# Reciprocals swapped between halves of the partitions, one row tile normalised before the last division, and own rows of the output projection interleaved

## The chip, the cores and the metric

The kernel runs on one core of a Trainium2 chip. The metric is the device time of one execution in microseconds. Five engines work beside each other: TensorE (PE, with its weight loads shown as PEld), VectorE (DVE), ScalarE (ACT), GpSimd (POOL) and SyncE (SP), which here only issues DMAs.

## The reference

x has 64 graphs of 256 nodes with 512 features; adj is one 256x256 graph for all of them. Two layers follow each other, each with a residual and a layer norm over the features:

```python
# layer 0
mi = einsum('bkd,od->bko', x, Wi);  mj = einsum('bkd,od->bko', x, Wj)
deg = adj.sum(axis=1)
x = layernorm(x + deg[None, :, None] * (mi + b) + einsum('ij,bjo->bio', adj, mj))
# layer 1: 8 heads of 64
q, k, v = split_heads(x @ Wq.T + bq), split_heads(x @ Wk.T + bk), split_heads(x @ Wv.T + bv)
scores = where(adj == 0, -inf, q @ k^T / 8)
attn = softmax(scores, axis=-1)
x = layernorm(x + concat_heads(attn @ v) @ Wo.T + bo)
```

## The kernel before, in words

**Tiles.** The 64 graphs are worked on in 32 groups g of two graphs. A graph has two row tiles of 128 nodes (t = 0, 1) and four chunks of 128 features (c = 0 to 3). The residual stream of a graph is xh[b], 128 partitions x 2 x 512.

**Main loop.** It has 31 trips. Trip g does the attention of group g and, between its steps, layer 0 of the two graphs of the next group (b1 and b2). Then come the output projection of group g and the values, queries and keys of group g+1. The order of instructions on each engine is the order in which the program calls the steps: `in_order` pins it. Every engine works through its own list, and semaphores hold it where it needs another engine's result. Pools of buffers add waits: a tile that takes a buffer waits for the last reader of the tile before.

**Three-part products.** A large product (values, queries, keys, output) is made from three fp32r products. Its left operand is split into a head (ACT, `split_head`, L665), a difference (DVE, `split_diff`, L668) and a low part (POOL or DVE, `split_low`, L671); the weights have been split in the same way into `factor` tiles, 768 KB each, which ACT's queue streams from DRAM through a ring of 6 (`bring`, L442). Heads and lows add up in one PSUM bank X, differences in another, Y (`rows_of_product`). ACT and DVE, or DVE alone, join the two: for the output projection, `add_x` (L811) and `add_y` (L815) add X and Y to xh. All matmuls have the line of a helper, L290, so one tells them apart by their tiles.

**Banks.** Pairs X, Y come from three places: "S" takes a score pair (pool of 2 pairs, tile pxy), "M" takes two of the 3 banks of the mm pool (px, py), and "A" takes one mm bank and the one value bank (py). The mm pool also serves layer 0 (po) and the denominators (den); the value bank also serves attention's output (pav).

**Parts of the attention output.** aoT holds the output of the group before the projection: four chunks, columns of graph 0 (own rows, n = 0, 1 by row tile) and of graph 1 (other rows, n = 2, 3). Its head lies in tile qT, its difference in kT, its low part in v, since those buffers are free then. Upper means chunks 0 and 1, lower chunks 2 and 3. Lower of graph 1 comes out of the last division of the trip.

**Division.** Softmax isn't normalised before the product with the values. `values` fills pav for two chunks; `divide_two` copies pav to aoT (ACT, L931) and calls `divide`. That sums each denominator over the keys on TensorE (den, 128 rows in groups of 32), takes the reciprocal on DVE (rden, L974), and spreads it with four DMAs of 64x256 from SBUF to SBUF (L979), so that each row of both chunks has its own reciprocal. SP issues the four, but in the last division of a trip ACT issues two of them. `multiply` then multiplies aoT by spread on POOL (L925). `total` sums rden on ACT for a check at the end.

**Normalisation and transposition of h.** `stat` takes the mean and variance of a row tile on DVE (L474 to L480) and the root on POOL (rstd, L482), and `give` scales the row tile on ACT (shift L487, xh L488). `send_h` stores the row tile to DRAM in column blocks (L687), `fetch_h` loads it back (hB, L692), and `turn_h` transposes it in blocks on DVE (hF, L506); SP issues both DMAs. h10 and h11 are row tiles 0 and 1 of b1. The row tiles of b2 are turned inside the output projection.

**The steps around the change**, in the order of the program: values 6 and 7 of the trip; low part of graph 0; statistics of row tile 1 of b2; last division; statistics of row tile 0; low part of graph 1, upper; scaling of both row tiles; store and fetch of both; then the output projection, with row 0, row 1 and the other rows as three steps, and the values product of the next group.

Of the kernel before, what the change touches and what calls it, by code (L numbers as in the profile page):

```python
# [16 lines left out]
P = 128  # L17
# [207 lines left out]
def unshifted_path(ctx, tc, flag, x, adj, wiT, wjT, b0, wqT, bq, wkT, bk, wvT, bv, woT, bo, out):  # L225
# [149 lines left out]
    def channels(q):  # L375

        half, j = divmod(q, 2)
        return slice(j * DH + half * R, j * DH + (half + 1) * R)

    def load_wo(t, c0):  # L380
        w = woT.rearrange("(c p) o -> p c o", p=P)
        for q in range(P // R):
            in_order(nc.sync.dma_start(out=t[q * R:(q + 1) * R], in_=w[channels(q), c0:c0 + t.shape[1], :]))

    def small_loads():
        with nc.allow_non_contiguous_dma(reason="512 numbers, once"):
            for q in range(P // R):
                in_order(nc.sync.dma_start(out=bv_t[q * R:(q + 1) * R],
                                           in_=bv.rearrange("r (c p) -> p (r c)", p=P)[channels(q)]))
        in_order(nc.sync.dma_start(out=bo_bc, in_=bo.to_broadcast([P, D])))  # L390
        return load_bias(bq, "bq"), load_bias(bk, "bk")

# [410 lines left out]
                    v_evict(g, i, t, banks[t])  # L803
        return run

    def o_steps(g, kinds, turn):
        parts = aoP[g]

        def add_x(i, t, banks):
            r = xh[NB * g + i][:, t, :]  # L810
            in_order(nc.vector.scalar_tensor_tensor(r, banks[0], UP, r, ALU.mult, ALU.add))  # L811

        def add_y(i, t, banks):
            r = xh[NB * g + i][:, t, :]
            in_order(nc.vector.tensor_add(r, banks[1], r))  # L815

        def one(t):
            def run():
                banks = pair(kinds[t])
                for which in ((0, 1), (2,)):  # L820
                    for c in range(NC):
                        rows_of_product(banks, parts, t, coming[c], c, which)
                add_x(0, t, banks)
                add_y(0, t, banks)
            return run

        def two():
            banks = [pair(kinds[NT + t]) for t in range(NT)]
            for c in range(NC):
                for which in ((0, 1), (2,)):  # L830
                    for t in range(NT):
                        rows_of_product(banks[t], parts, NT + t, coming[0], c, which)
# [8 lines left out]
            add_x(1, 0, banks[0])  # L841
            split_diff(*h1)
            add_y(1, 0, banks[0])
            add_x(1, 1, banks[1])
            add_y(1, 1, banks[1])
            split_three(*turn(0), nc.gpsimd)

        return [one(0), one(1), two]

    def finish_steps(g):  # L850

# [56 lines left out]
    def values(g, w):  # L908
        i, pr = divmod(w, NC)
        if w == 0:  # L910
            aoT[g] = p1.tile([P, NC, NB * N], F32, tag="aoT", name="aoT")
        pp = w % 2
        if pp == 0:
            pavs[g] = value_bank("pav").rearrange("p (r q) -> p r q", r=2)
        pe, _ = made[g, w]
        for kc in range(NT):
            for q in range(P // R):
                d0 = 2 * pr * DH + channels(q).start
                matmul(pavs[g][q * R:(q + 1) * R, pp, :], vv[g][:, i, kc, d0:d0 + R], pe[:, q % 2, kc, :],
                       start=(kc == 0), stop=(kc == NT - 1), tile_position=(0, q * R))  # L920

    def multiply():
# [4 lines left out]
    def divide_two(g, w):  # L927

        dst = target(g, w)
        last = w == NB * NC - 1 and g < NG - 1  # L930
        in_order(nc.scalar.copy(dst, pavs[g]))  # L931
        i, pr = divmod(w, NC)
        return divide(dst, [made.pop((g, w - 1))[1], made.pop((g, w))[1]],
                      rtot[:, NB * g + i, pr // 2:pr // 2 + 1], last)

    def total(rden, total_out):
        unused = p1.tile([P, N], F32, tag="unused", name="unused")
# [2 lines left out]
    def divide_at_once(g, w):  # L940


        den = score_bank("den").rearrange("p (r q) -> p r q", r=2)
        for pp in range(2):
            _, pk = made.pop((g, w - 1 + pp))
            for q in range(P // R):
                matmul(den[q * R:(q + 1) * R, pp, :], ones[:, :R], pk[:, q % 2, :], start=True, stop=True,
                       tile_position=(0, q * R))
# [12 lines left out]
        cols = slice(i * N, (i + 1) * N)  # L961
        return cut_parts(aoP[g], cs, cols), aoT[g][:, cs, cols]

    def divide(dst, pks, total_out, last):


        den = bank("den")[:, :N]
        for pp in range(2):
            for j in range(2):
                q = 2 * pp + j  # L970
                matmul(den[q * R:(q + 1) * R, :], ones[:, :R], pks[pp][:, j, :], start=True, stop=True,
                       tile_position=(0, q * R))
        rden = p1.tile([P, N], F32, tag="rden", name="rden")
        in_order(nc.vector.reciprocal(rden, den))  # L974
        spread = p1.tile([P, 2, N], F32, tag="spread", name="spread")
        for half in range(2):
            for pp in range(2):
# [131 lines left out]
    for g in range(NG - 1):  # L1109
# [214 lines left out]
```

## Time and profile before

| what | before |
|---|---|
| median of 3 runs | 2985.07 us (2984.91 to 2987.25) |
| the profiled execution | 2979.46 us, of which the span of the program's instructions is 2977.2 us |
| TensorE busy | 2934.5 us, 15694 matmuls, granted clock 0.998 |
| VectorE busy | 2310.1 us |
| GpSimd busy | 1273.0 us |
| ScalarE busy | 1194.6 us |
| DMA | 609.48 MB, 205 GB/s on average |

Busy times are sums over the whole span. Matmuls overlap each other in the records, so a busy TensorE is read by the distance from one start to the next, not by the length of a row. In a list of waits, each line names the engine and tile that waited, what ended the wait, the total in us, how often, and the longest. In a timeline, each row has its start in us, its length, the engine, the line, the operation with its tiles, and in brackets the idle time of the engine before it and who ended it.

### The profile page before, as it was taken

The numbers are of one execution on the slowest core, as the hardware profiler recorded it, in microseconds if no ns is written. First come the engines' busy times: TensorE is split into PE (matmuls) and PEld (weight loads), VectorE is DVE, ScalarE is ACT, GpSimd is POOL, SyncE is SP. The second block draws the span as 40 slices with busy tenths as digits, with TensorE's granted clock in tenths as the row PEclk, the third lists the DMA queues.
The fourth block names the chain that finished last, engine by engine and source line by source line (L and its number), as shares of the span: only waits on it lengthen the run. The fifth ranks groups of instructions, "written<-read, shape, count | busy, mean of one in ns | idle before, by whom it ended". The sixth has DMA issues, their size and how long they took to land. (4 is left out here: it accounts for less than half of the span.)

```text
span 2977.2 us, 42690 instructions
## 1 busy us (share of the span) xinstructions
PE 2934.5 (99%) x15694; PEld 1917.7 (64%) x15694; DVE 2310.1 (78%) x3497; ACT 1194.6 (40%) x2243; POOL 1273.0 (43%) x950
## 2 busy tenths in 40 slices
PE   9999999999999999999999999999999999999998
PEld 5566666666666666666666666666666666666655
DVE  5977787777887778877778777788777787777875
ACT  3433434434434334343343343443433434334333
POOL 3534444344444344443444444444434444344443
PEclk9999999999999999999999999999999999999999
DMA  6566655667555665556665566755566555666553
GB/s 230 172 231 237 217 162 185 222 234 240 178 179 197 235 239 202 167 188 229 236 237 164 177 211 231 245 184 170 197 237 238 201 160 191 232 237 236 166 167 125
DMA packets 305604, 609.48 MB, mean 205 GB/s; under 512 B 27632, under 2 KB 189424, under 8 KB 305136
## 3 DMA queue, kind: packets, MB, share of 16 engines
q10 hardware_dynamic: 75808, 391.02, 34.5%
q1 hardware_dynamic: 229584, 215.69, 25.1%
q8 instruction: 126, 2.06, 0.3%
q14 instruction: 86, 0.70, 0.1%
HBM read 494.67 MB, written 78.64 MB: 193 GB/s over the span
## 5 line engine op out<-in xcount | busy, mean ns | idle before, releaser
L897 POOL TENSOR_TENSOR pk<-pe 128x512 f32<-128x512 f32 x256 | 330.7, 1303 | 534.6 <-ACT pe L887 534.6
L290 PE MATMUL po<-w,xS 128*128 128x512 f32 x992 | 466.1, 602 | 1.5 <-DVE mj L570 1.5
L290 PE MATMUL po<-w,xT 128*128 128x512 f32 x808 | 387.4, 604 | 0.8 <-ACT u L549 0.8
L482 POOL TENSOR_TENSOR rstd<-ve,mhalf 128x1 f32<-128x1 f32 x256 | 155.3, 607 | 493.1 <-DVE below L480 491.9
L887 ACT ACTIVATE pe<-pe 128x1024 f32<-128x1024 f32 x256 | 270.6, 1057 | 148.2 <-DVE pe L883 148.2
L671 POOL TENSOR_TENSOR hL<-hF,hA 128x512 fp32r<-128x512 f32 x93 | 151.2, 1626 | 387.5 <-ACT hA L665 387.5
L290 PEld LDWEIGHTS po<-w,xS 128*128 128x128 f32 x992 | 177.8, 189 | 214.6 <-issue 162.2
L883 DVE TENSOR_TENSOR pe<-ps,maskT 128x1024 f32<-128x1024 f32 x256 | 300.9, 1196 | 3.6 <-PE ps L290 3.6
L759 DVE TENSOR_TENSOR kT<-py,kT 128x512 f32<-128x512 f32 x128 | 88.5, 691 | 259.7 <-ACT kT L758 259.7
L290 PEld LDWEIGHTS po<-w,xT 128*128 128x128 f32 x808 | 145.6, 189 | 180.5 <-issue 179.0
L367 POOL TENSOR_TENSOR xh<-xh,degb 128x1024 f32<-128x1024 f32 x64 | 152.4, 2382 | 254.9 <-DMA xh<-in_x_dram 134.8
L290 PE MATMUL ps<-qT,kT 64*128 64x256 f32 x2048 | 256.5, 389 | 0.0
L290 PE MATMUL pav<-pe,v_sb 128*32 128x256 f32 x4096 | 248.7, 382 | 3.5 <-DVE kT L759 1.5
L290 PEld LDWEIGHTS ps<-qT,kT 64*128 64x128 f32 x2048 | 187.0, 186 | 69.0 <-PE pav L290 38.7
L487 ACT ACTIVATE shift<-below,rstd 128x1 f32<-128x1 f32 x256 | 74.5, 291 | 386.3 <-POOL rstd L482 231.2
L974 DVE RECIPROCAL rden<-den 128x256 f32<-128x256 f32 x127 | 221.9, 1747 | 6.3 <-PE den L290 3.8
L290 PEld LDWEIGHTS pav<-pe,v_sb 128*32 128x32 f32 x4096 | 118.3, 109 | 155.4 <-issue 49.2
L488 ACT ACTIVATE xh<-xh,shift,rstd 128x512 f32<-128x512 f32 x256 | 208.9, 816 | 8.5
L925 POOL TENSOR_TENSOR aoT<-aoT,spread 128x512 f32<-128x512 f32 x127 | 205.7, 1620 | 6.9 <-DMA spread<-rden 5.9
L665 ACT ACTIVATE hA<-hF 128x512 fp32r<-128x512 f32 x124 | 77.8, 628 | 287.1 <-DVE hF L506 231.5
L290 PE MATMUL px<-hA,factor 128*128 128x512 f32 x640 | 184.3, 410 | 0.0
L290 PE MATMUL py<-hD,factor 128*128 128x512 f32 x640 | 176.3, 397 | 2.2 <-ACT kT L758 2.2
(142 smaller groups left out, 6060.1 us busy)
## 6 DMA issues: line engine op xcount, KB each, us to landing
factor<-wv ACTq DMA_DIRECT2D x124, 768.0 KB, 6.3
factor<-wq ACTq DMA_DIRECT2D x124, 768.0 KB, 6.6
factor<-wk ACTq DMA_DIRECT2D x124, 768.0 KB, 6.4
factor<-wo ACTq DMA_DIRECT2D x120, 768.0 KB, 7.2
xB<-in_x_dram SPq DMA_DIRECT2D x256, 128.0 KB, 3.7
xh<-in_x_dram SPq DMA_DIRECT2D x64, 512.0 KB, 8.9
h_cols<-xh SPq DMA_DIRECT2D x124, 256.0 KB, 2.3
hB<-h_cols SPq DMA_DIRECT2D x124, 256.0 KB, 3.1
```

Of the source, the lines that this page charges most:

```text
L290: in_order(nc.tensor.matmul(*args, **kw))
L367: in_order(nc.gpsimd.tensor_tensor(xh[b], xh[b], degb, ALU.add))
L482: order(nc.gpsimd.tensor_tensor(rstd, ve, mhalf, ALU.pow))
L488: order(nc.scalar.activation(t, t, AF.Identity, bias=shift, scale=rstd))
L665: in_order(nc.scalar.activation(parts[0], src, AF.Identity, scale=DOWN))
L671: in_order(engine.tensor_tensor(parts[1], src, parts[0].bitcast(F32), ALU.subtract))
L759: in_order(nc.vector.tensor_add(dst, Y, dst))
L883: in_order(nc.vector.tensor_add(pe.rearrange("p j t q -> p j (t q)"), ps.rearrange("p j t q -> p j (t q)"), maskT.rearrange("p t q -> p (t ...
L887: in_order(nc.scalar.activation(flat, flat, AF.Exp, scale=QSCALE, accum_out=etot[:, NB * g + i, pr:pr + 1]))
L897: in_order(nc.gpsimd.tensor_tensor(pk, pe[:, :, 0, :], pe[:, :, 1, :], ALU.add))
L925: in_order(nc.gpsimd.tensor_tensor(d, d, spread, ALU.mult))
L974: in_order(nc.vector.reciprocal(rden, den))
```

## The change

**Reciprocals.** In half of the rows (those of the second half of each head, q = 2 and 3) the two chunks of a pair change places in aoT: `values` writes chunk `pp ^ (q // 2)`. So each row's own reciprocal for one chunk comes out of the reciprocal in place. The reciprocal is written straight into the first half of the tile spread, and two DMAs of 64x256 fill the second half by exchanging the upper and the lower 64 partitions. In the last division of a trip, SP issues one and ACT the other. The rows of wo and of the value bias are loaded in the same swapped order, once at the start, and wo once more at the end (`chunk_sets`). In the last group, the reciprocal of the second division takes the buffer of another tile.

**Normalisation.** Row tile 1 of b2 is scaled, and its store issued, around the last division and not after the statistics of row tile 0. The low part of graph 0 is made in two pieces, upper before and lower after the root of row tile 1. The fetch of row tile 0 comes after the splits of h10.

**Output projection.** The own rows are one step of TensorE with its matmuls interleaved, and their adds are called apart. Both own rows take score pairs, the other rows take "A" and "M"; of the values products of the next group, the first takes two score pairs, the second "A" and "M". The turn of h10 on DVE comes after the adds of row 0.

```diff
     def load_wo(t, c0):
         w = woT.rearrange("(c p) o -> p c o", p=P)
+        n = t.shape[1]
         for q in range(P // R):
-            in_order(nc.sync.dma_start(out=t[q * R:(q + 1) * R], in_=w[channels(q), c0:c0 + t.shape[1], :]))
+            for to, of in chunk_sets(q):
+                in_order(nc.sync.dma_start(out=t[q * R:(q + 1) * R, to:n:2 if q > 1 else 1],
+                                           in_=w[channels(q), c0 + of:c0 + n:2 if q > 1 else 1, :]))
...
-        def one(t):
-            def run():
-                banks = pair(kinds[t])
-                for which in ((0, 1), (2,)):
-                    for c in range(NC):
-                        rows_of_product(banks, parts, t, coming[c], c, which)
-                add_x(0, t, banks)
-                add_y(0, t, banks)
-            return run
+        def own():
+            for n, cs in ((0, (0, 1)), (1, (2, 3))):
+                banks[n] = pair("S")
+                times(n, range(NC), (0, 1))
+                times(0, cs, (2,))
+            times(1, range(NC), (2,))
+
+        def adds(n):
+            add_x(n)
+            add_y(n)
+
+        def others():
+            banks.update({2: pair("A"), 3: pair("M")})
...
-                matmul(pavs[g][q * R:(q + 1) * R, pp, :], vv[g][:, i, kc, d0:d0 + R], pe[:, q % 2, kc, :],
+                matmul(pavs[g][q * R:(q + 1) * R, pp ^ (q // 2), :], vv[g][:, i, kc, d0:d0 + R], pe[:, q % 2, kc, :],
...
-        rden = p1.tile([P, N], F32, tag="rden", name="rden")
+        spread = p1.tile([P, 2, N], F32, tag="lo" if other else "spread", name="spread")
+        rden = spread[:, 0, :]
         in_order(nc.vector.reciprocal(rden, den))
-        spread = p1.tile([P, 2, N], F32, tag="spread", name="spread")
         for half in range(2):
-            for pp in range(2):
-                issuer = nc.scalar if last and pp else nc.sync
-                in_order(issuer.dma_start(out=spread[half * DH:(half + 1) * DH, pp, :],
-                                          in_=rden[pp * DH:(pp + 1) * DH, :]))
+            issuer = nc.scalar if last and half else nc.sync
+            in_order(issuer.dma_start(out=spread[half * DH:(half + 1) * DH, 1, :],
+                                      in_=spread[(1 - half) * DH:(2 - half) * DH, 0, :]))
...
-            v = [v_pair(g, 0, "MS"[::-1], False), v_pair(g, 1, "AS", True)]
+            v = [v_pair(g, 0, "SS", False), v_pair(g, 1, "AM", True)]
...
-        split_low(*ao_parts(g, 0, every), nc.gpsimd)
+        split_low(*ao_parts(g, 0, upper), nc.gpsimd)
         stat2(1)
+        give2(1)
+        split_low(*ao_parts(g, 0, lower), nc.gpsimd)
         total_up = divide_two(g, 7)
+        send_h(b2, 1)
         stat2(0)
         split_low(*ao_parts(g, 1, upper), nc.gpsimd)
-        give2(1)
         give2(0)
         total_up()
-        send_h(b2, 1)
         send_h(b2, 0)
         fetch_h(b2, 1)
-        fetch_h(b2, 0)
         split_diff(*ao_parts(g, 1, upper))
         if g + 2 < NG:
             next_p[0][2]()
+        own, adds, others = o_steps(g, lambda t: turn_h(b2, t))
+        own()
+        adds(0)
         h10 = turn_h(b1, 0)
         multiply()
         split_head(*ao_parts(g, 1, lower))
         split_head(*h10)
+        fetch_h(b2, 0)
         p, q = next_p, next_q
         v, q_, k = projection_steps(g + 1)
         end = finish_steps(g)
-        o = o_steps(g, "SMAS", lambda t: turn_h(b2, t))
-        o[0]()
         split_diff(*ao_parts(g, 1, lower))
         split_low(*ao_parts(g, 1, lower), nc.vector)
         split_diff(*h10)
         split_low(*h10, nc.vector)
-        o[1]()
-        run([o[2], v[0]])
+        adds(1)
+        others()
+        v[0]()
```

More of the change, by code (lines that the diff above doesn't have):

```diff
@@ L378, in channels, with chunk_sets @@
         return slice(j * DH + half * R, j * DH + (half + 1) * R)
+    def chunk_sets(q):
+        return ((0, 1), (1, 0)) if q > 1 else ((0, 0),)
     def load_wo(t, c0):
         w = woT.rearrange("(c p) o -> p c o", p=P)
+        n = t.shape[1]
         for q in range(P // R):
-            in_order(nc.sync.dma_start(out=t[q * R:(q + 1) * R], in_=w[channels(q), c0:c0 + t.shape[1], :]))
+            for to, of in chunk_sets(q):
+                in_order(nc.sync.dma_start(out=t[q * R:(q + 1) * R, to:n:2 if q > 1 else 1],
+                                           in_=w[channels(q), c0 + of:c0 + n:2 if q > 1 else 1, :]))
     def small_loads():
@@ L387, in small_loads @@
             for q in range(P // R):
-                in_order(nc.sync.dma_start(out=bv_t[q * R:(q + 1) * R],
-                                           in_=bv.rearrange("r (c p) -> p (r c)", p=P)[channels(q)]))
+                for to, of in chunk_sets(q):
+                    step = 2 if q > 1 else 1
+                    in_order(nc.sync.dma_start(out=bv_t[q * R:(q + 1) * R, to:NC:step],
+                                               in_=bv.rearrange("r (c p) -> p (r c)", p=P)[channels(q), of:NC:step]))
         in_order(nc.sync.dma_start(out=bo_bc, in_=bo.to_broadcast([P, D])))
@@ L804, in v_pair, with o_steps, times, add_x @@
         return run
-    def o_steps(g, kinds, turn):
+    def o_steps(g, turn):
         parts = aoP[g]
[L809 to L815, printed above, removed]
-        def one(t):
-            def run():
-                banks = pair(kinds[t])
-                for which in ((0, 1), (2,)):
-                    for c in range(NC):
-                        rows_of_product(banks, parts, t, coming[c], c, which)
-                add_x(0, t, banks)
-                add_y(0, t, banks)
-            return run
-        def two():
-            banks = [pair(kinds[NT + t]) for t in range(NT)]
+        banks = {}
+        r = {n: xh[NB * g + n // NT][:, n % NT, :] for n in range(NB * NT)}
+        def times(n, cs, which):
+            for c in cs:
+                rows_of_product(banks[n], parts, n, coming[c], c, which)
+        def add_x(n):
+            in_order(nc.vector.scalar_tensor_tensor(r[n], banks[n][0], UP, r[n], ALU.mult, ALU.add))
+        def add_y(n):
+            in_order(nc.vector.tensor_add(r[n], banks[n][1], r[n]))
+        def own():
[9 more added lines that the diff above has]
+            banks.update({2: pair("A"), 3: pair("M")})
             for c in range(NC):
                 for which in ((0, 1), (2,)):
-                    for t in range(NT):
-                        rows_of_product(banks[t], parts, NT + t, coming[0], c, which)
+                    for n in (2, 3):
+                        rows_of_product(banks[n], parts, n, coming[0], c, which)
                 coming.pop(0)
@@ L840, in two @@
                     split_low(*h1, nc.gpsimd)
-            add_x(1, 0, banks[0])
+            add_x(2)
             split_diff(*h1)
-            add_y(1, 0, banks[0])
-            add_x(1, 1, banks[1])
-            add_y(1, 1, banks[1])
+            add_y(2)
+            adds(3)
             split_three(*turn(0), nc.gpsimd)
-        return [one(0), one(1), two]
+        return own, adds, others
     def finish_steps(g):
@@ L933, in divide_two @@
         return divide(dst, [made.pop((g, w - 1))[1], made.pop((g, w))[1]],
-                      rtot[:, NB * g + i, pr // 2:pr // 2 + 1], last)
+                      rtot[:, NB * g + i, pr // 2:pr // 2 + 1], last, g == NG - 1 and w == 3)
     def total(rden, total_out):
@@ L943, in divide_at_once @@
         den = score_bank("den").rearrange("p (r q) -> p r q", r=2)
-        for pp in range(2):
-            _, pk = made.pop((g, w - 1 + pp))
+        pks = [made.pop((g, w - 1 + pp))[1] for pp in range(2)]
+        for s in range(2):
             for q in range(P // R):
-                matmul(den[q * R:(q + 1) * R, pp, :], ones[:, :R], pk[:, q % 2, :], start=True, stop=True,
-                       tile_position=(0, q * R))
+                matmul(den[q * R:(q + 1) * R, s, :], ones[:, :R], pks[s ^ (q // 2)][:, q % 2, :], start=True,
+                       stop=True, tile_position=(0, q * R))
         inverses = p1.tile([P, 2, N], F32, tag="spread", name="rden")
@@ L962, in ao_parts, with divide @@
         return cut_parts(aoP[g], cs, cols), aoT[g][:, cs, cols]
-    def divide(dst, pks, total_out, last):
+    def divide(dst, pks, total_out, last, other):
         den = bank("den")[:, :N]
@@ L972, in divide @@
                        tile_position=(0, q * R))
-        rden = p1.tile([P, N], F32, tag="rden", name="rden")
+        spread = p1.tile([P, 2, N], F32, tag="lo" if other else "spread", name="spread")
+        rden = spread[:, 0, :]
         in_order(nc.vector.reciprocal(rden, den))
-        spread = p1.tile([P, 2, N], F32, tag="spread", name="spread")
         for half in range(2):
-            for pp in range(2):
-                issuer = nc.scalar if last and pp else nc.sync
-                in_order(issuer.dma_start(out=spread[half * DH:(half + 1) * DH, pp, :],
-                                          in_=rden[pp * DH:(pp + 1) * DH, :]))
+            issuer = nc.scalar if last and half else nc.sync
+            in_order(issuer.dma_start(out=spread[half * DH:(half + 1) * DH, 1, :],
+                                      in_=spread[(1 - half) * DH:(2 - half) * DH, 0, :]))
         products.append((dst, spread))
```

## The prediction

> **What bounds the kernel now.** The page comes first: which engine is full?
>
> ```profile
> PE 2934.5 (99%) x15694; PEld 1917.7 (64%) x15694; DVE 2310.1 (78%) x3497; ACT 1194.6 (40%) x2243; POOL 1273.0 (43%) x950
> ```
>
> TensorE is busy for 99% and its instructions don't change in number, so only its waits can give time. The second view is the list of waits. It charges most of them to PEld, because a matmul's wait holds its weight load first:
>
> ```profile
> PEld pxy L290 <- POOL v L671: 19.8, 31, 1.3
> ...
> PEld py L290 <- DVE xh L815: 14.0, 31, 0.5
> ...
> PEld px L290 <- DMA factor<-wv: 10.0, 16, 1.4
> ...
> PE pxy L290 <- DVE xh L815: 7.9, 4, 3.1
> ...
> PEld py L290 <- DVE kT L668: 2.7, 6, 0.5
> ```
>
> Two waits come 31 times, once in each trip of the main loop; the others come in some trips. The third view is the timeline around one output projection. I take the trip whose first projection matmul starts at 1880.29, and call that moment 0. (All the starts of the 31 trips were laid over each other; 15 or so agree with this one within 0.1 us.)
>
> ```profile
> 1880.43 2.39 POOL L671 TENSOR_TENSOR v<-aoT,qT 128x1024 fp32r<-128x1024 f32 x1
> 1881.60 1.76 DVE L974 RECIPROCAL rden<-den 128x256 f32<-128x256 f32 x1
> 1884.29 0.68 DVE L668 SCALAR_TENSOR_TENSOR kT<-qT,aoT 128x512 fp32r<-128x512 f32 x1
> 1884.39 0.99 POOL L482 TENSOR_TENSOR rstd<-ve,mhalf 128x1 f32<-128x1 f32 x1 [1.06 <-DVE below L480]
> 1885.36 1.31 POOL L671 TENSOR_TENSOR v<-aoT,qT 128x512 fp32r<-128x512 f32 x1
> 1886.62 1.28 POOL L925 TENSOR_TENSOR aoT<-aoT,spread 128x512 f32<-128x512 f32 x1
> 1887.94 0.63 ACT L665 ACTIVATE qT<-aoT 128x512 fp32r<-128x512 f32 x1 [0.77 <-POOL aoT L925]
> 1888.60 0.69 DVE L668 SCALAR_TENSOR_TENSOR kT<-qT,aoT 128x512 fp32r<-128x512 f32 x1 [0.64 <-ACT qT L665]
> 1891.73 0.69 DVE L815 TENSOR_TENSOR xh<-py,xh 128x512 f32<-128x512 f32 x1
> ```
> ```profile
> 1882.88 0.76 PEld L290 LDWEIGHTS pxy<-factor,v 128*128 128x128 f32 x4 [0.61 <-POOL v L671]
> 1892.48 0.19 PEld L290 LDWEIGHTS py<-factor,hD 128*128 128x128 f32 x1 [0.43 <-DVE xh L815]
> ```
>
> Matmuls of this stage start every 0.227 us. Wait A: the ninth needs the low part (tile v) of which POOL writes all four chunks in one piece of 2.39 us; it starts at +2.59 and not at +2.25 (0.34), and the interval after it is 0.34 (0.11 more): 0.45 us. Wait B: the second matmul of the next values product needs a bank that the last add of row 1 (L815, to 1892.42) gives back: 0.18 + 0.11 = 0.29 us. The chain between is the important part of the picture: reciprocal, statistics, POOL rstd, POOL split, POOL multiply, ACT head, DVE difference run end to end to +9.00. The matmul that needs this difference (number 37, counted from 0) starts at +9.30 without waiting. It has 0.1 to 0.2 us in hand.
>
> **The Trainium skill.** "TensorE: Matmul & The Clock Gate", LDWEIGHTS, says that a load takes its columns divided by 1.2: 107 ns for 128. The trace agrees in its own way: the rows say 188 ns, but after every stall the next interval is longer by 0.108 to 0.114. So a wait costs its length plus 0.11. "SBUF — State Buffer", Who interferes with whom, says that a VectorE instruction with two SBUF inputs and a GpSimd one that reads SBUF exclude each other. The trace agrees: this rstd takes 0.99 beside the difference of 1884.29, the one 1.6 us earlier 0.54. "DMA: Bandwidth & Descriptors", Issuing engines are not separate DMA queues, says that a second issuing engine saves only issue time. Here that is what counts: ACT's two issues of spread hold it for 1.15 us (1883.39 to 1884.54), and its next instruction starts at 1884.59.
>
> **The change part by part.**
>
> *Split of the low part, rstd between, own rows interleaved.* POOL does two chunks (mean of the 128x512 form: 1.30), rstd 0.54, two chunks 1.30: upper half ready at +1.45, lower at +3.3. The new order asks for them at matmul 8 (+2.25) and matmul 18 (about 2.25 + 10 x 0.227 = +4.5). Wait A goes: -0.45.
>
> *What is late next.* The chain to +9.00 doesn't move. Its POOL work keeps its order from the second rstd on, and that rstd starts when DVE's second statistics end (+4.08); nothing ahead of it on DVE is taken away. Without A, matmul 37 would start at 9.30 - 0.45 = +8.85. It waits for +9.00 + 0.06 (the time from a release to a start in wait B) and pays 0.11: +0.32. Net of A and this: -0.13.
>
> *Banks.* Own rows both take score pairs; the next values product takes two score pairs: the first was freed by adds(0), the second by adds(1), which end at +12.14 as before, but is asked for by matmul 51 and not 49. Matmul 51 comes at 9.06 + 0.34 + 13 x 0.227 = +12.35; 12.14 + 0.06 + 0.11 is just earlier. Wait B goes: -0.29. The other rows now take all three mm banks, at +6.1 to +6.5. The last of them is freed by DVE's L540 add at 1885.64 (+5.35): hidden, with 0.7 in hand. The following values pair then waits for the first add of the last row, not for its second: 0.7 us easier.
>
> *Reciprocals.* 2 DMAs of 64x256 for 4 in each of 127 divisions; where SP issues all of them, its 2.38 us become about 1.2. In the last division SP and ACT issue one each. POOL's multiply starts right behind its split (1886.62) with the last landing at +6.0, so on the path this brings nothing. The reciprocal now writes the tile that the previous multiply reads. That multiply ended at 1880.47, the reciprocal starts at 1881.60: hidden, with 1.1 us in hand.
>
> *Normalisation and copies.* Row 1's shift and scaling (0.29 + 0.81 on ACT) come before the copy of pav: copy done near +3.7, needed by the multiply at +6.33. ACT's only issue is then at about +3.7, landing near +5.7: in time. SP stores row 1 at +3.7 (before: +5.47), row 0 at +6.3 (+6.5), and fetches row 1 back at about +6.9 (+7.84), ahead of the two 768 KB factor loads and not among them. Row 0's fetch, put later, still stands behind its store on SP. These loads are what varies: 31 trips take 91.55 us on average, and trips without an extra wait 90.70. The 0.85 x 30 = 25 us are: late fetches that hold L815 and so the score bank (about 12, from four trips), factor loads of wv (about 7), trips in which the chain to +9.00 is late (2.6), the rest. The first should nearly go, the second stays mostly (the load is issued up to 0.45 earlier, and asked for 0.36 earlier), the third stays. I take -14.
>
> *Once.* Start: 2 more DMAs of bv and 4 more of wo on SP, 0.56 each, 3.4 us of issue, behind them nothing that PE waits for before 60 us. End: 2 more for wo_sb, landed long before. Nothing, at most +1.
>
> Sum: 31 x (-0.13 - 0.29) = -13; -14; -27 us together. The profiled execution took 2979.46 (span 2977.2 and 2.3 around it) and gives 2952; the median of the runs, 2985.07, lies 5.6 higher, so **2958**.
>
> Bounds of what the trace doesn't show: the new wait at matmul 37 is between 0 (if ACT, freed of one issue, or POOL bring the multiply 0.3 earlier: 10 us more gain) and 0.45 (4 us less); the varying part between -25 and +5 (other trips may be hit once SP's stream is shorter).
>
> **Rivals.** *Both waits go for good*: the chain ends 0.4 earlier and most late loads go. For it: the shorter issues; against it: POOL is back to back from 1884.39 to 1887.90 and DVE starts the chain. 31 x 0.74 + 18 = 41: 2944. *The wv loads become the gate*: TensorE arrives earlier at matmul 66 and waits for the same landing (+15.5 to +16.1 in ordinary trips; asked for at 9.06 + 0.34 + 28 x 0.227 = +15.76). For it: ten trips wait there already; against it: two of the competing transfers start earlier. Gain 31 x 0.1 + 5 = 8: 2977. *Slower*: the reciprocal's new wait for POOL decides. What it is late is late at matmul 37, and queued behind it on DVE are the second statistics, the L540 add that frees the mm bank, and the adds of row 0. The gain of 27 / 31 = 0.9 us per trip is eaten when the multiply ends 2.0 us later than traced (1.1 in hand + 0.9); at 2.5 it is 31 x 0.5 = 15: 3000. Against it: that multiply is behind only POOL's pair sums and gets its reciprocals sooner. *It doesn't do what it says*: the interleaving only moves A to matmul 37 and B to 51: within 4 us, 2984.
>
> **How the numbers follow.** Main case 0.52 (2958), both gone 0.2, loads 0.14, moved only 0.09, slower 0.05. What a measurement can tell from no change is 0.2%, 6 us. Two thirds of the loads case are still faster by more: 0.86 faster, 0.09 same, 0.05 slower. Range 2941 to 2976.
>
> **What would show it.** Right: no wait of pxy for POOL v; none of the values product for L815; a wait of py for the kT difference (L668 before) in nearly every trip, 0.4 to 0.5 long in the list of waits; the four waits of 1 to 3 us for L815 gone. Wrong: the reciprocal idle for POOL, matmul 37 never waiting, or wv waits in most trips.

## The result and the profile after

The changed kernel takes 2952.23 us (median of 4 runs, 2948.72 to 2953.39), the kernel before beside it 2985.06 (4 runs, 2984.91 to 2987.25): a ratio of 0.9891, 95% interval 0.9877 to 0.9906. The profiled execution took 2951.62 us with a span of 2949.8; the span of before was 2977.2, so 27.4 us are gone. The median fell by more, 32.8 us: the profiled execution of before was 5.6 us faster than its median, that of the changed kernel 0.6.

TensorE is still the full engine, on the page of the changed kernel:

```profile
PE 2919.3 (99%) x15694; PEld 1915.4 (65%) x15694; DVE 2319.2 (79%) x3497; ACT 1198.7 (41%) x2243; POOL 1277.3 (43%) x981
```

In its list of waits (us in total, how often, the longest) the lines of POOL's v and of the adds L815 have left the output projection. In their places stand one wait that comes 31 times and one that comes in some trips:

```profile
PEld py L290 <- DVE kT L677: 14.3, 31, 0.5
...
PEld pxy L290 <- DMA factor<-wv: 12.7, 23, 1.3
...
PE pxy L290 <- DMA factor<-wv: 4.7, 11, 0.9
```

The list counts every weight load and matmul that is held, however briefly; in 12 trips the wait for wv delays a matmul by 0.3 to 1.0 us.

This is the timeline of the changed kernel in the trip that corresponds to the one shown of before. Its moment 0 is 1863.03. (L988 is the reciprocal, L677 a difference, L680 a low part, L938 the multiply, L696 the stores and L701 the fetches of h, L451 a factor load. A row of SPq with x2 begins at the first of its two issues.)

```profile
1863.17 1.29 POOL L680 TENSOR_TENSOR v<-aoT,qT 128x512 fp32r<-128x512 f32 x1
...
1864.31 1.76 DVE L988 RECIPROCAL spread<-den 128x256 f32<-128x256 f32 x1
...
1864.93 1.30 POOL L680 TENSOR_TENSOR v<-aoT,qT 128x512 fp32r<-128x512 f32 x1
...
1866.68 2.96 SPq L696 DMA_DIRECT2D h_cols<-xh  x2
...
1869.32 1.29 POOL L938 TENSOR_TENSOR aoT<-aoT,spread 128x512 f32<-128x512 f32 x1
...
1869.75 2.34 SPq L701 DMA_DIRECT2D hB<-h_cols  x2
...
1870.82 0.33 ACTq L451 DMA_DIRECT2D factor<-wv  x1
...
1871.31 0.69 DVE L677 SCALAR_TENSOR_TENSOR kT<-qT,aoT 128x512 fp32r<-128x512 f32 x1 [0.59 <-ACT qT L674]
...
1872.06 0.19 PEld L290 LDWEIGHTS py<-factor,kT 128*128 128x128 f32 x1 [0.46 <-DVE kT L677]
```

The split of the low part comes in two pieces, the multiply starts at +6.29 (before +6.33), and the kT difference ends at +8.97. Matmul 37 waits for it and starts at +9.03. Row 1 is stored at +3.65 and not +5.47. Its fetch is issued at +6.72 and not +7.84; the first wv load goes at +7.79 (before +7.91). The experiments turn on the distance between these last two. I call it the **lead**, positive when the fetch goes first.

From trip 1 to trip 31 there are 30 intervals. Their mean was 91.51 us (the prediction had 91.55) and is 90.66; a trip without an extra wait took 90.70 and takes 90.33. The constant part gave 0.37 x 30 = 11.1 us. The varying part gave (0.81 - 0.33) x 30 = 14.4.

Most of before's varying part, 15.7 of 24.4 us, lies in four trips, those whose moments 0 are 320.6, 1054.3, 1695.0 and 2333.8. In each of them a store of h is late (see the last section), and row 1's fetch lands at +14.8 to +16.6, where the median of the other trips is +11.8. The experiments call them the **four trips**. In the changed kernel no fetch of row 1 lands past +12.

### The profile page after: what moved, and what is told of

Read it like the earlier page. It is cut to its first block, busy times and chain, and to the rows that moved or that the text cites. A ratio compares the mean times of both kernels' runs of the same rounds, so it can differ in the third digit from the quotient of the medians.

```text
span 2949.8 us, 42319 instructions
## 1 busy us (share of the span) xinstructions
PE 2919.3 (99%) x15694; PEld 1915.4 (65%) x15694; DVE 2319.2 (79%) x3497; ACT 1198.7 (41%) x2243; POOL 1277.3 (43%) x981
## 2 busy tenths in 40 slices
DMA packets 285410, 592.81 MB, mean 201 GB/s; under 512 B 23696, under 2 KB 169232, under 8 KB 284944
## 5 line engine op out<-in xcount | busy, mean ns | idle before, releaser
L680 POOL TENSOR_TENSOR hL<-hF,hA 128x512 fp32r<-128x512 f32 x93 | 151.1, 1624 | 367.5 <-ACT hA L674 367.5
L988 DVE RECIPROCAL spread<-den 128x256 f32<-128x256 f32 x127 | 222.2, 1749 | 3.8 <-PE den L290 3.0
L938 POOL TENSOR_TENSOR aoT<-aoT,spread 128x512 f32<-128x512 f32 x127 | 206.2, 1623 | 0.1
```

What stands on the lines that cost most here:

```text
L680: in_order(engine.tensor_tensor(parts[1], src, parts[0].bitcast(F32), ALU.subtract))
L938: in_order(nc.gpsimd.tensor_tensor(d, d, spread, ALU.mult))
```

## The experiments

All were timed against the kernel before on the same chip. "Landing" is that of row 1's fetch, as the median over the first 30 trips, counted from moment 0.

| kernel | us (median) | ratio, 95% interval | lead | landing |
|---|---|---|---|---|
| before | 2985.06 | | +0.07 | +11.86 |
| changed | 2952.23 | 0.9891 (0.9877 to 0.9906) | +1.05 | +9.67 |
| reciprocals alone | 2960.32 | 0.9925 (0.9911 to 0.9938) | +0.74 | +9.92 |
| normalisation alone | 2965.55 | 0.9948 (0.9934 to 0.9962) | +0.68 | +10.01 |
| rows and banks alone | 2976.61 | 0.9982 (0.9972 to 0.9992) | -0.03 | +13.17 |
| reciprocals alone, ACT held | 2994.10 | 1.0035 (1.0023 to 1.0047) | -0.06 | +13.14 |
| reciprocals alone, extra transfers | 2962.37 | 0.9930 (0.9918 to 0.9942) | +0.68 | +10.00 |
| before, loads behind the fetch | 2958.44 | 0.9919 (0.9905 to 0.9932) | +0.42 | +10.52 |
| changed without normalisation | 2956.09 | 0.9906 (0.9889 to 0.9922) | +0.60 | +9.92 |
| changed without reciprocals | 2952.17 | 0.9899 (0.9882 to 0.9917) | +0.68 | +9.88 |
| changed, old banks | 2957.51 | 0.9920 (0.9906 to 0.9933) | +1.29 | +9.66 |
| changed, earlier split | 2948.86 | 0.9887 (0.9871 to 0.9902) | +1.05 | +10.02 |
| changed, loads on SP | 2942.57 | 0.9861 (0.9846 to 0.9876) | +0.70 | +9.68 |
| changed, both of these | 2931.98 | 0.9829 (0.9815 to 0.9842) | +0.55 | +10.03 |

### The parts, one at a time

**Reciprocals alone**: before, with the new layout and nothing else.

```diff
-            for pp in range(2):
-                issuer = nc.scalar if last and pp else nc.sync
-                in_order(issuer.dma_start(out=spread[half * DH:(half + 1) * DH, pp, :],
-                                          in_=rden[pp * DH:(pp + 1) * DH, :]))
+            issuer = nc.scalar if last and half else nc.sync
+            in_order(issuer.dma_start(out=spread[half * DH:(half + 1) * DH, 1, :],
+                                      in_=spread[(1 - half) * DH:(2 - half) * DH, 0, :]))
```

> The kernel before with the new layout of the reciprocals alone (swapped chunks, two DMAs for four in each division). My theory: the chain recip, statistics, root, split, multiply is bound by DVE and POOL and not by the landing of spread, so TensorE's two standing waits (POOL v L671 and the adds of row 1, 31 times each) stay: 2984, between 2981 and 2986; only trips in which spread lands later than POOL can get better, at most 3 us together. Rival (the shorter DMA issues carry the change): 2972 or less, and fewer late factor loads. Rival (the reciprocal's new wait for POOL costs): over 2988, with the reciprocal idle for POOL aoT.

Measured: 2960.32, which is 22.6 us better than before's 2982.96 in these runs. My theory, that this part brings nothing, fell. Waits A and B stay in every trip and an undisturbed trip still takes 90.7. What goes is the varying part: there is no long wait for the adds of the other rows (L815 in before), and only wv loads are waited for in some trips (0.1 to 0.9 us):

```profile
PEld px L290 <- DMA factor<-wv: 8.5, 13, 1.2
```

Row 1 is stored at +4.84 instead of +5.47 and its fetch issued at +7.18. In the trace the 30 intervals gain 16.2 us, of which 14.3 come from the four trips.

**Normalisation alone**: before, with the scaling, the stores and the fetches in their new places.

```diff
         stat2(1)
+        give2(1)
         total_up = divide_two(g, 7)
+        send_h(b2, 1)
         stat2(0)
         split_low(*ao_parts(g, 1, upper), nc.gpsimd)
-        give2(1)
         give2(0)
         total_up()
-        send_h(b2, 1)
         send_h(b2, 0)
         fetch_h(b2, 1)
-        fetch_h(b2, 0)
...
         split_head(*h10)
+        fetch_h(b2, 0)
```

> The kernel before with the normalisation of row tile 1 and its store put ahead, and the fetch of row tile 0 put later; low part in one piece, rows, banks and reciprocals as before. My theory: the two standing waits stay, but the fetch of row tile 1 comes about 1 us earlier and lands ahead of the factor loads, so the four trips with a wait of 1 to 3 us for the adds lose it: 2985 - 12 = 2973, between 2968 and 2978. Rival (those trips come from where the program's stream happens to be interrupted, and not from the fetch): 2985 within 4, with about as many late trips elsewhere.

Measured: 2965.55, a larger gain than expected, and again out of the varying part: the four trips gain 14.6 us, all others together lose 0.7, as an undisturbed trip takes 90.88 here, 0.18 more than before. The store starts at +4.37 and the fetch is issued at +7.26. The four DMAs of spread are still there, and in about six trips the chain to the kT difference is late.

**Rows and banks alone**: the changed kernel with the old reciprocals and everything of the normalisation in its old place.

```diff
-        give2(1)
         split_low(*ao_parts(g, 0, lower), nc.gpsimd)
         total_up = divide_two(g, 7)
-        send_h(b2, 1)
         stat2(0)
         split_low(*ao_parts(g, 1, upper), nc.gpsimd)
+        give2(1)
         give2(0)
         total_up()
+        send_h(b2, 1)
         send_h(b2, 0)
         fetch_h(b2, 1)
+        fetch_h(b2, 0)
...
-            issuer = nc.scalar if last and half else nc.sync
...
+            for pp in range(2):
+                issuer = nc.scalar if last and pp else nc.sync
...
```

> The kernel after with the old reciprocals (four DMAs) and the old place of normalisation, store and fetches: what stays is the split of the low part, the interleaved own rows and the new banks. My theory: both standing waits go, one of 0.32 for the lower kT difference comes in each trip (0.37 us per trip net, 11 to 13 us), and late fetches hurt less since the next values pair waits for an earlier add: 2985 - 15 = 2970, between 2965 and 2975. Rival (interleaving only moves the waits): 2983 or more. If the parts add up, e1, e2 and this one together give the 33 us of the whole change.

Measured: 2976.61, less gain than expected. Waits A and B are gone, but this line in the kernel's list of waits is new:

```profile
PEld px L290 <- POOL hL L671: 24.4, 28, 1.0
```

The trip got shorter ahead of the first wv load, so ACT issues it at +7.81, 0.03 ahead of the fetch (+7.84). The fetch lands at +13.2, DVE turns the row late, and POOL's low part hL comes too late for matmul 86 in 28 trips. The interleaving's gain had become this wait.

The three gains, each against before's 2982.96, add up to 22.6 + 17.4 + 6.4 = 46.4 us, where the whole change is worth 33. The first two buy the same thing: nearly all of either gain lies in the same four trips.

### What the reciprocals and the normalisation have in common

Theory now: both bring row 1's store forward. The layout does so because ACT issues one transfer and not two and starts the scaling that much earlier. What counts is whether the fetch goes well ahead of the first wv load or beside it. Rival: fewer transfers and fewer packets (285,410 for 305,604).

**Reciprocals alone, ACT held**: the time of the missing issue is put back, without a transfer.

```diff
         products.append((dst, spread))
         if last:
+            held = p1.tile([P, N], F32, tag="held", name="held")
+            for half in range(2):
+                in_order(nc.scalar.copy(held, bo_bc[:, half * N:(half + 1) * N]))
             return lambda: total(rden, total_out)
```

> The kernel with the new reciprocals alone (2960.3), with two more copies of 128x256 on ACT right behind its one issue of the last division; they stand in for the issue that the new layout takes away (0.35 to 0.4 each by the row of a 128x256 activation) and move no data between memories. Theory: the 22.5 us of that kernel came from ACT alone: one issue less, row 1 is normalised 0.6 earlier, its store starts at +4.84 and not +5.47, its fetch is issued at +7.18 and not +7.84, ahead of the first wv load of +7.94. Held again, the store is back at +5.4 to +5.6, the fetch is issued at about +7.9 and lands at +11 and later, the L815 bank waits are back in some trips: 2981 us (2975 to 2986). Rival: fewer and fewer-packet transfers were the gain, and they are still fewer here: 2961 us (2957 to 2965).

Measured: 2994.10, slower than before. The whole gain is gone and 9 us more, although the transfers are still the fewer ones. The copies hold ACT a little longer than the missing issue did: row 1 is stored at +5.58, 0.11 later than before. The fetch goes at +7.97, 0.06 behind the wv load. The long waits for the adds are back, now together with a shorter one for hL in most trips (L824 is the second add, L680 the low part):

```profile
PE pxy L290 <- DVE xh L824: 11.3, 8, 3.1
...
PEld px L290 <- POOL hL L680: 10.8, 24, 0.5
```

Against the reciprocals alone, the 30 intervals of the trace lose 31 us: 15.9 in the four trips, 15.1 in the others.

**Reciprocals alone, extra transfers**: SP's issues and the traffic are put back in all divisions but a trip's last one.

```diff
+        if not last and not other:
+            extra = p1.tile([P, N], F32, tag="extra", name="extra")
+            for half in range(2):
+                in_order(nc.sync.dma_start(out=extra[half * DH:(half + 1) * DH, :],
+                                           in_=spread[(1 - half) * DH:(2 - half) * DH, 0, :]))
         products.append((dst, spread))
```

> The kernel with the new reciprocals alone (2960.3), with two more transfers of 64x256 into a tile that nobody reads, issued by SP in every division but the last one of a trip, so that SP's stream and the traffic are there as before (four transfers per division). Theory (only ACT's time in the last division counts): no change, 2961 us (2957 to 2965), store of row 1 still at about +4.84. Rival (the traffic, or SP's stream of issues): most of the gain goes, 2972 to 2983 us.

Measured: 2962.37, as with the reciprocals alone. The page counts 300,612 packets. So SP's issues and the traffic of the other divisions don't matter. The run with ACT held kept the fewer transfers in every division and lost the gain; the rival is out.

**Before, loads behind the fetch**: nothing of the change is in this kernel. Only the order of the transfers is another: SP issues the two loads, and `fetch` is row 0's fetch_h, which no longer stands right behind row 1's.

```diff
                 if c:
-                    bring()
+                    bring(issuer=nc.sync if c == 1 else None)
                 if c == 1:
-                    bring()
+                    bring(issuer=nc.sync)
+                    fetch()
```

> The kernel before, with one thing changed: the two wv loads are issued by SP, behind row 1's fetch, and row 0's fetch behind them. No reciprocal, normalisation, row or bank is touched; row 1 is stored at +5.47 and its fetch issued at +7.84 as before, but the first wv load now comes after it (+8.4) and not 0.1 behind it on another engine. Theory (the order of these two transfers is what the varying part hangs on): the fetch lands near +10.5 instead of +11 to +16.6, the L815 bank waits of 2 to 3 us go, waits A and B stay in every trip: 2966 us (2960 to 2973). Rival (the order does not matter, the sum of the bytes does): row 1 still lands past +11.5, 2980 us or more.

Measured: 2958.44, at the lower end of what the theory said, 25.5 us better than the 2983.90 of before in these runs. Its list of waits still has A and B in full; of the loads little is left, and the 3 us waits for L815 are gone:

```profile
PEld pxy L290 <- POOL v L671: 19.8, 31, 1.3
...
PEld py L290 <- DVE xh L815: 13.8, 31, 0.5
...
PEld px L290 <- DMA factor<-wv: 4.6, 8, 1.6
```

So most of the varying part hangs on the order of two transfers. Trip by trip, the 30 intervals gain 19.0 us, 14.2 of them in the four trips. A store of h is late in such trips of this kernel just as in before, but here the loads wait behind the fetch, and such a trip costs 0 to 0.8 us instead of 2.3 to 5.2. (This kernel also takes two issues of 0.33 us off ACT; an undisturbed trip takes 90.7 as before, so in such a trip that brings nothing.)

In most of the other 26 trips of before the lead of 0.07 was still enough: 15 take 90.7 us or hardly more, with the fetch landing at +11.2 to +12.4. It had no margin, though. At a lead of -0.03 (rows and banks alone) or -0.06 (ACT held) the fetch lands near +13.2, and most trips wait for hL. A larger lead gains little in an ordinary trip: 1.9 us over all 26 with the reciprocals alone. With the reciprocals alone, what counts is that row 1's store takes at most 2.6 us even in the four trips; a store 2 us late would have used up the lead of 0.74. Why it escapes there is not tried; the last section has what the traces show.

The next four fences show one ordinary trip each: the DMA view of a stretch of about 1 us in which both are issued (name, queue, count, KB each, us from issue to landing). First before, where the fetch is issued 0.07 ahead of the load:

```profile
factor<-wv ACTq DMA_DIRECT2D x1, 768.0 KB, 5.1
hB<-h_cols SPq DMA_DIRECT2D x1, 256.0 KB, 4.0
```

Reciprocals alone, 0.72 ahead in this trip:

```profile
factor<-wv ACTq DMA_DIRECT2D x1, 768.0 KB, 5.4
hB<-h_cols SPq DMA_DIRECT2D x1, 256.0 KB, 2.7
```

ACT held, 0.08 behind in this trip:

```profile
factor<-wv ACTq DMA_DIRECT2D x1, 768.0 KB, 4.9
hB<-h_cols SPq DMA_DIRECT2D x1, 256.0 KB, 5.0
```

Loads behind the fetch, 0.42 ahead:

```profile
factor<-wv SPq DMA_DIRECT2D x1, 768.0 KB, 4.3
hB<-h_cols SPq DMA_DIRECT2D x1, 256.0 KB, 2.6
```

The same 256 KB take 2.7, 4.0 or 5.0 us, by where the issue stands within 0.8 us. The Trainium skill ("DMA: Bandwidth & Descriptors", Issuing engines are not separate DMA queues) says that DMAs of all issuing engines interleave on the same 16 engines; the 4.0 and 5.0 beside the load agree with that. It adds that the issue time saved by a second issuing engine is usually small beside the transfer. That is so here (ACT's two issues take 1.15 us, its one issue 0.51), and it still decided more than 20 us of the kernel.

### What each part is worth once the other is there

**Changed without normalisation** (reciprocals, rows and banks):

```diff
-        give2(1)
         split_low(*ao_parts(g, 0, lower), nc.gpsimd)
         total_up = divide_two(g, 7)
-        send_h(b2, 1)
         stat2(0)
         split_low(*ao_parts(g, 1, upper), nc.gpsimd)
+        give2(1)
         give2(0)
         total_up()
+        send_h(b2, 1)
         send_h(b2, 0)
         fetch_h(b2, 1)
+        fetch_h(b2, 0)
```

> The changed kernel with row 1's normalisation, store and fetch and row 0's fetch put back to their old places. Theory: ACT's one issue less already brings the fetch of row 1 to about +7.2, 0.6 ahead of the first wv load (+7.8), so the move of the normalisation adds nothing to it: 2952 us (2948 to 2957), as the changed kernel. Rival: the 0.4 us by which the move goes further count; then hL of row 0 is waited for at matmul 86, and it takes 2959 us or more.

**Changed without reciprocals** (normalisation, rows and banks), the four transfers back:

```diff
-            issuer = nc.scalar if last and half else nc.sync
-            in_order(issuer.dma_start(out=spread[half * DH:(half + 1) * DH, 1, :],
-                                      in_=spread[(1 - half) * DH:(2 - half) * DH, 0, :]))
+            for pp in range(2):
+                issuer = nc.scalar if last and pp else nc.sync
+                in_order(issuer.dma_start(out=spread[half * DH:(half + 1) * DH, pp, :],
+                                          in_=rden[pp * DH:(pp + 1) * DH, :]))
```

> The changed kernel with the old layout of the reciprocals (four transfers per division, two of them by ACT in the last). Theory: the normalisation ahead of the last division brings the fetch of row 1 in front of the first wv load without the new layout, so most of the gain stays; ACT's second issue makes the chain to the kT difference late in about six trips (1 us each, as with the normalisation alone): 2957 us (2952 to 2963). Rival: the new layout is needed for it, 2970 us or more.

Measured: 2956.09 and 2952.17; the changed kernel takes 2952.23, and the intervals of the three ratios overlap. Either part alone is enough for the median. With both, the lead is 1.05 instead of 0.6 to 0.7, and that has a use that the medians hardly show. Without the one or the other, in four of 30 trips row 1's fetch still lands past +12; in the worst, matmul 73 waits 1.7 us for a bank of the other rows (L825) and matmul 86 0.9 for hL. Such a trip costs 3.5 to 3.8 us, and comes three times without the normalisation and once without the reciprocals: row 1's store is late, and a lead of 0.6 to 0.7 doesn't cover that. With both there is none.

**Changed, old banks**: only the pools of the pairs are as before.

```diff
-                banks[n] = pair("S")
+                banks[n] = pair("SM"[n])
...
-            banks.update({2: pair("A"), 3: pair("M")})
+            banks.update({2: pair("A"), 3: pair("S")})
...
-            v = [v_pair(g, 0, "SS", False), v_pair(g, 1, "AM", True)]
+            v = [v_pair(g, 0, "MS"[::-1], False), v_pair(g, 1, "AS", True)]
```

> The kernel after with the old choice of banks (own rows S and M, other rows A and S, values M with S and A with S). My theory: the wait of the values product's second matmul for the adds of row 1 comes back in each trip, 0.29 x 31 = 9 us: 2961, between 2957 and 2966; the wait for the kT difference stays or is a little shorter if row 1 waits for its bank. Rival (the banks do nothing once rows are interleaved): 2952 within 3.

Measured: 2957.51. In its list of waits, B is back (L828 is the second add), and with it a wait that nobody had foretold: row 1's second bank comes from the mm pool, where the denominators still lie until the reciprocal has read them.

```profile
PEld py L290 <- DVE xh L828: 16.4, 31, 0.5
...
PEld py L290 <- DVE spread L988: 12.7, 30, 0.4
...
PEld py L290 <- DVE kT L677: 5.0, 29, 0.4
```

The new wait at matmul 11 costs 0.15 to 0.19 and 0.11, and takes most of the place of that at 37. An undisturbed trip is 90.70 again, so, with the rows interleaved, the banks are worth the whole 0.37 per trip. The total still rises by only 5.3 us, since fewer trips wait for wv: the varying part is 2.4 us here and 9.9 in the changed kernel.

### Two steps further

**Changed, earlier split**: POOL splits the second row's upper half ahead of the second rstd.

```diff
-        stat2(0)
         split_low(*ao_parts(g, 1, upper), nc.gpsimd)
+        stat2(0)
```

> The changed kernel with POOL's split of the upper half of the second row put ahead of the second rstd. Theory: the multiply then starts about +5.4 instead of +6.29, the kT difference ends near +8.4 instead of +8.98, the wait at matmul 37 (0.20 to 0.23 and 0.11, 31 times, 10 us) goes; the wv load of matmul 66 is then asked for 0.32 earlier and takes back the gain in the 12 trips that wait for it now and tips some more: 2946 us (2942 to 2950). Rival: row 0's normalisation, now later by up to 1.3 on POOL, makes its store and fetch late, so that hL of that row becomes a wait: 2952 us or more.

**Changed, loads on SP**: the wv loads of the other rows' loop are issued by SP with row 0's fetch behind them, as in the diff above.

> The changed kernel with the two wv factor loads of the other rows' loop issued by SP and no longer by ACT, and row 0's fetch behind them in SP's stream. Theory: the fetch (256 KB of the 1.8 MB that are under way together, about 1.1 us at 235 GB/s) no longer shares the engines with the second load, which lands near +14.5 instead of +15.4 to +16.9; the waits on wv (12 trips, 0.3 to 1.0 each, some 10 us with the small ones) go: 2943 us (2939 to 2947). Rival: the fetch lands after +16.4, where DVE's turn of row 0 takes it, hL follows late and the matmuls that need it near +20.5 wait: 2950 us or more.

**Changed, both of these**:

> The changed kernel with both of the last two edits: the split of the second row's upper half ahead of the second rstd (alone 2948.9), and the wv loads issued by SP with row 0's fetch behind them (alone 2942.6). Theory: without the wait at matmul 37 the load of matmul 66 is asked for at +15.4; it landed at +14.2 to +16.0 with the loads first, so some nine trips wait 0.1 to 0.6, 3 us together, of the 10 that the wait at 37 costs: 2935 us (2931 to 2940). Rival: row 0's fetch lands past +16.4 more often and hL of that row is waited for at matmul 86: 2942 us or more.

Measured: 2948.86, 2942.57 and 2931.98. With the earlier split the wait at 37 is gone, but the load is waited for in more trips; this is the line in its list of waits:

```profile
PEld pxy L290 <- DMA factor<-wv: 17.2, 25, 1.1
```

With the loads on SP, the second of them lands at +14.97 (median) instead of +15.74, and row 0's fetch, now behind it, at +15.63 instead of +15.53. The same line there:

```profile
PEld pxy L290 <- DMA factor<-wv: 1.7, 5, 0.5
```

With both, neither wait comes in most trips: an undisturbed trip takes 90.0, and 2931.98 is 20 us better than the changed kernel.

## Why the prediction was right, and where it was not

Predicted 2958 us, measured 2952.23. For the profiled execution the sum gave 2952, and it took 2951.62; the span fell by 27.4 us where the sum said 27. The prediction then added the 5.6 us by which before's median lay above its profiled execution, and in the changed kernel that distance is 0.6.

- **Wait A and what is late next: right.** The wait at matmul 37 came 31 times. From start to start it is 0.20 to 0.23 and 0.11, where the prediction had 0.32 in all.
- **Banks: right in effect, incomplete in the cause.** Wait B is gone. The constant part gave 0.37 per trip where the sum had 0.42. From start to start the three waits give 0.43; 0.06 is lost again at matmul 480, a denominator's, which waits that much longer for POOL (pk) in the kernels with the new reciprocals. With the old banks a second wait, at matmul 11, would have come, which the prediction did not see.
- **Reciprocals, "on the path this brings nothing": this step failed.** It followed only the landing of spread to POOL's multiply. The prediction itself had read that ACT's two issues hold it for 1.15 us and that its next instruction starts right after; it did not follow that instruction to the store, to the fetch and to the wv load. Alone, the step is worth 22.6 us. The sum survived because the normalisation, counted at -14, buys the same thing: with it in place the reciprocals bring nothing that these runs can tell. That was luck; nothing in the prediction says that the two overlap.
- **The varying part, -14: right in sum (14.4), not in its terms.** The late fetches went, as said; the four trips held 15.7 us (prediction: about 12), and one of their four waits for L815 was 0.4 us and not 1 to 3. The late chain (2.6) was to stay and went: in no trip of the changed kernel is the kT difference later than its standing +9.0. The waits for wv were to stay mostly, at less than 7 us; they now make up nearly all of what is left, 0.33 x 30 = 10 us.
- **The rival of the wv loads as the gate** holds in 12 trips (0.3 to 1.0 us each), not in most; the 23 times in the list are mostly shorter. It was the limit for the next step: the earlier split alone gave only 3 us of 10.
- **Once:** expected 0 to +1. Outside the 30 intervals the span fell by 27.4 - 25.5 = 1.9 us. The first moment 0 comes at 139.27 (before 139.23), so this lies behind the last one: in the 31st projection wait A was 1.06 us from start to start, and with it B and a wait for wv went. TensorE is 2.2 us ahead there and loses 0.4 again.
- **What was missing in the method:** the prediction knew that the fetch would go "ahead of the two loads and not among them", and priced this by the four worst trips. For the gain that was sound, since they hold most of it. What it lacked was the margin: with a lead of 0.07 us in an ordinary trip, a change that lets the wv load go a tenth earlier, or the fetch a tenth later, costs 0.3 to 0.8 us in most trips. The rows and banks alone did that.

## What to carry to other kernels

When two transfers of different urgency are issued by different engines at about the same moment, measure the lead between the issues before anything else; a tenth of a microsecond can be the difference between a transfer alone and one that shares, and a late producer of the urgent one uses up the lead. Put the urgent one and the bulky one on one engine in that order, so that the order no longer hangs on time. Price parts of a change with and without each other: what looks like three gains can be one gain twice and a new wait.

## What the runs showed of the hardware

**The lead against a large transfer acts in steps of tenths of a microsecond.** Over the kernels of the table, a fetch of 256 KB issued 0.03 to 0.06 us behind a load of 768 KB takes 5.2 us to its landing; 0.07 ahead of it, 4.0; from 0.42 ahead on, 2.7 to 3.0 (medians).

**One packet of an instruction queue goes with a late store.** The four trips of before with an L815 wait of 0.4 to 3.3 us are the very ones in which a store of h took 3.5 us or more; in the others none took over 2.8. In each of them, and in no other, one 16 KB packet of the instruction queue q8 starts while the stores are under way. In three of them row 1's store is late, in that at 1054.3 row 0's alone; there the fetch goes at +7.83 as usual but lands at +14.8. The trip at 320.6 (stores 5.5 to 10.6 us after its moment 0), in the DMA view of before:

```profile
q8 instruction: 1, 0.02, 1.5%
issues: line engine op xcount, KB each, median us to landing
...
h_cols<-xh SPq DMA_DIRECT2D x2, 256.0 KB, 4.3
```

The trip at 1880.3, the same stretch, with no such packet:

```profile
issues: line engine op xcount, KB each, median us to landing
...
h_cols<-xh SPq DMA_DIRECT2D x2, 256.0 KB, 2.3
```

The store is 2 us late, the fetch is then issued at +9.96, behind both wv loads, and DVE and TensorE wait in turn (timeline of before):

```profile
337.23 1.14 DVE L506 STREAM_TRANSPOSE hF<-hB 128x512 f32<-128x512 f32 x1 [4.44 <-DMA hB<-h_cols]
...
341.82 0.77 PE L290 MATMUL pxy<-factor,hA 128*128 128x512 f32 x1 [3.10 <-DVE xh L815]
```

The kernel with the loads behind the fetch has four such trips too (row 1's store landing at +9.4 to +9.8) and no long L815 wait in them; there the loads queue behind the fetch. That the packet is the cause was not tried; the four matches, and the same match in the changed kernel without normalisation (six late stores, six packets), are what there is. The match is not general: in the changed kernel three stores of row 1 take 3.3 to 3.5 us with no packet of q8.

In reciprocals alone the packet is there too, at +6.8 to +7.4 in five trips. Row 0's store takes 3.2 to 4.5 us in them, but row 1's, issued 0.63 earlier than in before, at most 2.6. In the changed kernel without normalisation, with row 1's store at the same +4.84, the packet comes at +5.7 to +5.9 in four trips, and the store takes 3.4 to 3.9. So what an earlier store is worth hangs on where the packet falls, and that differs from kernel to kernel. One such trip costs 2.3 to 5.2 us in before, so a difference of some us between two of these kernels may be no more than that.

**After some long waits of TensorE the granted clock is halved for a while.** In before, around the waits of 3.10 and 2.60 us in two of the four trips, the granted clock is 0.50 for 3.41 us (from 341.4 and from 2355.3), and matmuls of the same kind start every 0.427 us instead of 0.227: about 1.6 us more per trip. The wait of 1.93 us has none. With ACT held it is the same in two trips (waits of 2.56 and 3.10), but not in a third (3.09). The main loop of the changed kernel has no such stretch. Over the 36 executions of before that the experiments timed, the five with a mean clock of 0.996 took 2984.2 to 2990.4 us, the 15 with 0.998 or 0.999 took 2977.9 to 2985.9; that these halvings make the difference was not traced.
